# A row of zeros between the parts of queries and keys and the shift, so that two kinds of matmul contract 33 and 35 rows

## The chip, the core and the metric

The kernel runs on one core of one Trainium2 chip. The metric is the device time of one execution in microseconds. The core's engines are TensorE (PE; its weight loads stand in the trace as an engine of their own, PEld), VectorE (DVE), ScalarE (ACT), GpSimd (POOL) and SyncE (SP, which here only issues DMAs). Each works through its own queue in order; they wait for each other by semaphores.

## The reference

One transformer layer: a layer norm, causal attention with 16 heads of 8 dimensions on 8 sequences of 512 tokens, and beside it, on the same normed input, a mixture of 8 experts of which 2 are taken per token, with a shared expert. Everything is float32.

```python
def _L0_attn_ref(x, W1, b1, Wp, bp):
    h = x @ W1 + b1
    h = jnp.swapaxes(h.reshape(B, S, H, 3 * d), 1, 2)
    q, k, v = (h[..., :d], h[..., d:2 * d], h[..., 2 * d:])
    w = jnp.einsum('bhqd,bhkd->bhqk', q, k) / dk
    mask = jnp.tril(jnp.ones((S, S), dtype=x.dtype))
    w = jax.nn.softmax(w * mask - (1.0 - mask) * NEG_BIG, axis=-1)
    a = jnp.einsum('bhqk,bhkd->bhqd', w, v)
    a = jnp.swapaxes(a, 1, 2).reshape(B, S, E)
    return a @ Wp + bp
...
xn = _layernorm(x, axis=-1)
x = x + attn(xn) + (shared expert + the two chosen experts, weighted)(xn)
```

## The kernel before

**Queries and keys.** For a sequence b, `project_qk` makes queries and keys of all heads, each split into a high and a low part (`parts`, L225 and L226), which go through DRAM (`store_qk`) and come back (`fetch`, L259 and L260) into `qs` and `ks`: tiles of 128 partitions in which two heads lie side by side, one from partition 0, one from partition 64 (`SIDE`). Of each head's 64 partitions the first 32 (`QK`) hold the parts: high and low times 8 dimensions, in the order in which one contraction over 32 rows gives the full product. Rows 32 and 33 hold the shift: in `ks` two rows of ones, set once at the start by `memset` on POOL (L137, six of them: three buffers, two heads each); in `qs` the negative row maximum as a high and a low part, written by four DMAs per group of heads (`put_shift`, L394).

**Two passes of scores.** The work is cut into 32 groups (`n`) of four heads and each group into five tiles of scores (`TILES`): two "wide", two "mixed", one "half", which makes 160 steps. In each the same scores are made twice. `peak_scores` (L324, PSUM tile `sc`) contracts the 32 rows of parts; DVE takes the row maxima (L354, L359, L363, L364). `fill` (L278, PSUM tile `scT`) contracts 34 rows with queries and keys swapped, so that transposed scores less the maximum come out; ACT takes the exponential (L405). In each of these two calls two heads are worked on together, one in the array's rows from 0, the other in those from 64. The maxima run nine steps (`AHEAD`) ahead of the exponentials.

The masks: tiles 0 and 2 of the maxima (`MASKED_TILES`) find the mask in PSUM already, copied there by ACT (`prepare`, L312). Of the transposed scores the mask is added on PE (L294) or, in the steps with `on_pool` (from step 25, `BUSY`, until all routed experts are stored), put to zero by POOL after the exponential (L413).

**The order of a step** is written out by hand for PE, DVE, ACT and SP (`manual_schedule`); POOL's order is the framework's. On PE a step goes: `fill` of this step (L278, with L294 where not `on_pool`); `peak_scores` of the step nine further on (L324); a piece of the experts (`extra`: L545, and from `side` L563, L529 and others); and the weighted sums of an earlier tile (`attend`, L428):

```python
waiting.append((kind, j, weigh(n, kind, j, on_pool)))
parts_then = look(step + AHEAD) if step + AHEAD < total_steps else lambda: None
if step not in alone:
    extra()
```

`sc` and `scT` have one buffer each (`m_ps`, `w_ps`).

**The start.** After layer norm of the first sequence and its queries and keys come `project_v(0)`, whose DVE instruction L247 writes the values into `v_ext`, and then the norms of the other sequences. `v_ext` (two tiles) is first set to zero by POOL (L139), and those memsets stand in the program after the ones on `ks`.

Of the kernel before, what the change touches and what calls it, by code (L numbers as in the profile page):

```python
# [10 lines left out]
F32 = mybir.dt.float32  # L11
# [43 lines left out]
QK = 4 * D  # L55
SIDE = 64
# [3 lines left out]
def attn_moe_kernel(  # L60
# [15 lines left out]
    nc = tc.nc  # L76
# [44 lines left out]
    for i in range(NV):  # L121
        t = const.tile([P, NC, H, 32], F32, name=f"v_ext{i}")
# [5 lines left out]
    qs, ks = [], []  # L128
    for i in range(NU):
        q = const.tile([P, HP, S], F32R, name=f"qs{i}")  # L130
        k = const.tile([P, HP, S], F32R, name=f"ks{i}")
        qs.append(q)
        ks.append(k)

    for k in ks:
        for at_ in (QK, SIDE + QK):
            nc.gpsimd.memset(k[at_ : at_ + 2].bitcast(F32), 1.0)  # L137
    for t in v_ext:
        nc.gpsimd.memset(t, 0.0)  # L139
        nc.gpsimd.memset(t[:, :, :, D : D + 1], 1.0)  # L140
# [122 lines left out]
    def rows_of(n, jj, rows):  # L263
        u, i, t = n // 2 % NU, n % 2 * 2 + jj // 2, jj % 2
        at_ = slice(SIDE * t, SIDE * t + rows)
        return qs[u][at_, i, :], ks[u][at_, i, :]
# [4 lines left out]
    def fill(n, kind, j, bare):  # L271

        ps = w_ps.tile([P, 2, S], F32, name="scT")

        def part(out_, jj, width, first):
            q, k = rows_of(n, jj, QK + 2)
            i = NC - width // P
            nc.tensor.matmul(  # L278
                out_, lhsT=k[:, ts(i, P)], rhs=q[:, i * P :], start=first, stop=True,
                skip_group_check=True,  # L280
            )

        if kind == "half":
            blocks = [(u * 2 * P, 2 * P) for u in range(2)]
        else:
            blocks = [(0, S)] if kind == "wide" else [(0, 3 * P), (3 * P, P)]
        for at_, width in blocks:
            for t in range(2):
                jj = (at_ // P if kind == "half" else j) + t
                part(ps[:, t, at_ : at_ + width], jj, width, at_ == 0)  # L290
        if not bare:
            for at_, _ in blocks:
                for t in range(2):
                    nc.tensor.matmul(  # L294
                        ps[:, t, at_ : at_ + P], lhsT=ident16, rhs=mask_k, start=False, stop=True,
                        skip_group_check=True,
                    )
        return ps
# [19 lines left out]
    def peak_scores(n, i):  # L318
        ready_ = bool(ahead)
        ps = ahead.pop() if ready_ else m_ps.tile([P, 2, S], F32, name="sc")  # L320

        def part(at_, jj, c, key, count, start):
            q, k = rows_of(n, jj, QK)
            nc.tensor.matmul(  # L324
                ps[:, jj % 2, ts(at_, P) if count == 1 else ds(at_ * P, count * P)],
                lhsT=q[:, ts(c, P)], rhs=k[:, key * P : (key + count) * P],
                start=start, stop=True, skip_group_check=True,
            )

        j = i // 2 * 2  # L330
        if i == 4:
            blocks = [(0, 0, 2, 0, 2, True), (2, 2, 2, 0, 2, False)]
        elif i in MASKED_TILES:
            blocks = [(c, j, c, c, 1, not ready_ and c == 0) for c in range(NC)]
        else:
            blocks = [(0, j, 3, 0, 3, True), (3, j, 1, 0, 1, False)]
        for at_, jj, *rest in blocks:
            for t in range(2):
                part(at_, jj + t, *rest)
        if i in MASKED_TILES and not ready_:  # L340
            for t in range(2):
                nc.tensor.matmul(
                    ps[:, t].rearrange("p (b k) -> p b k", k=P), lhsT=ident16,
                    rhs=mask_q.unsqueeze(1).to_broadcast([P, NC, P]), start=False, stop=True,
                    skip_group_check=True,
                )
        return ps
# [32 lines left out]
    def shift(n, parts):  # L380

        ps = misc([32, P], "mT_ps")
        nc.tensor.transpose(
            ps, parts.rearrange("p t r i c -> p (t r i c)").bitcast(F32), ident
        )
        mT = at.tile([32, P], F32R, name="mT")
        nc.vector.tensor_copy(mT, ps)
        return partial(put_shift, n, mT)

    def put_shift(n, mT):  # L390
        for t in range(2):
            for r in range(2):
                row = SIDE * t + QK + r
                nc.sync.dma_start(  # L394
                    qs[n // 2 % NU][row : row + 1, ts(n % 2, 2), :].rearrange(
                        "o i (c s) -> o (i c) s", s=P
                    ).bitcast(F32),
                    mT[ts(2 * t + r, 8)].bitcast(F32),
                )
# [631 lines left out]
```

## Time and profile before

| | |
|---|---|
| runs | 672.35 us, the median of 3 (669.31 to 675.39) |
| profiled execution | 672.46 us, of which the span from the first to the last instruction is 670.8 us |
| PE busy | 607.0 us (91%) |
| DVE, ACT, POOL busy | 450.4, 352.7, 223.6 us |
| mean granted PE clock | 0.921 |
| from 130 to 570 us | PE busy 421.02 of 440 us, granted clock 0.98 |

Busy PE includes the time in which a matmul's result is still on its way, so 91% is not a measure of the array's use. In the views, "34*128" is the number of rows that a matmul contracts times the columns of its weights, and "34x384" rows times moving columns. "The chain of work that ended last" is followed back from the last instruction, at each step to what released it.

### The profile page before, as it was taken

The numbers are of one execution on the slowest core, as the hardware profiler recorded it, in microseconds if no ns is written. First come the engines' busy times: TensorE is split into PE (matmuls) and PEld (weight loads), VectorE is DVE, ScalarE is ACT, GpSimd is POOL, SyncE is SP. The second block draws the span as 40 slices with busy tenths as digits, with TensorE's granted clock in tenths as the row PEclk, the third lists the DMA queues.
The fourth block names the chain that finished last, engine by engine and source line by source line (L and its number), as shares of the span: only waits on it lengthen the run. The fifth ranks groups of instructions, "written<-read, shape, count | busy, mean of one in ns | idle before, by whom it ended". The sixth has DMA issues, their size and how long they took to land.

```text
span 670.8 us, 13319 instructions
## 1 busy us (share of the span) xinstructions
PE 607.0 (91%) x4830; PEld 433.9 (65%) x4830; DVE 450.4 (67%) x1059; ACT 352.7 (53%) x582; POOL 223.6 (33%) x325
## 2 busy tenths in 40 slices
PE   3699889998999899998999899989999899989882
PEld 1576657665777577766776677757777677666451
DVE  6547586775777767765776577765777577769643
ACT  3232344554566646665675566664666466535340
POOL 9400077777521111211111112111111111566774
PEclk9556798998999999999999899999999999979986
DMA  8970151416747676657747675857565753111252
GB/s 264 250 203 1 64 171 53 115 53 218 200 159 202 194 208 183 181 178 243 201 148 190 215 194 166 201 194 221 164 178 185 241 160 78 42 47 45 63 136 64
DMA packets 65218, 105.16 MB, mean 157 GB/s; under 512 B 7808, under 2 KB 36224, under 8 KB 65152
## 3 DMA queue, kind: packets, MB, share of 16 engines
q1 hardware_dynamic: 49440, 86.40, 43.2%
q0 software_dynamic: 5344, 13.12, 6.8%
q10 hardware_dynamic: 10368, 4.79, 2.6%
q8 instruction: 39, 0.64, 0.4%
q14 instruction: 27, 0.22, 0.1%
HBM read 71.24 MB, written 32.51 MB: 155 GB/s over the span
## 4 chain that ended last, share of the span: by engine, by line
PE 78%; DVE 10%; ACT 5%; issue 3%; DMA 3%; SPq 0%; DVEq 0%; ACTq 0%
PE gu L545 25%; PE sc L324 12%; PE av L428 11%; PE y L563 11%; PE scT L278 9%; PE lg L734 2%; PE ot L461 2%; ACT th L550 2%; PE scT L294 1%; ACT sc L312 1%; PE s_ps L529 1%; DVE th L551 1%; DMA results<-o 1%; PE qk_ps L224 1%; DVE x_sb L631 1%
## 5 line engine op out<-in xcount | busy, mean ns | idle before, releaser
L405 ACT ACTIVATE pT<-scT 128x1024 f32<-128x1024 f32 x160 | 164.2, 1026 | 125.2 <-PE scT L294 63.9
L413 POOL TENSOR_SCALAR_AFFINE_SELECT pT<-pT 128x256 f32<-128x256 f32 (+1 forms) x156 | 66.3, 438 | 327.9 <-ACT pT L405 324.9
L545 PE MATMUL gu<-sT,w 128*128 128x128 f32 x864 | 125.9, 289 | 2.3 <-PE sc L324 2.1
L359 DVE TENSOR_REDUCE diag<-sc 128x8 f32<-128x1024 f32 x64 | 78.3, 1223 | 66.8 <-PE sc L324 50.5
L545 PEld LDWEIGHTS gu<-sT,w 128*128 128x128 f32 x864 | 105.5, 192 | 14.4 <-PE sc L324 3.5
L550 ACT ACTIVATE th<-gu 128x256 f32<-128x256 f32 x156 | 59.8, 383 | 80.5 <-PE gu L545 78.6
L324 PE MATMUL sc<-ks,qs 32*128 32x128 f32 (+2 forms) x896 | 95.2, 315 | 4.6 <-ACT sc L312 3.5
L551 DVE SCALAR_TENSOR_TENSOR th<-th,gu 128x256 f32<-128x256 f32 x156 | 65.6, 420 | 48.7 <-ACT th L550 48.1
L428 PE MATMUL av<-pT,v_ext 128*32 128x512 f32 (+3 forms) x1024 | 92.4, 457 | 0.0
L278 PE MATMUL scT<-qs,ks 34*128 34x384 f32 (+3 forms) x512 | 83.8, 379 | 6.1 <-ACT pT L405 3.3
L324 PEld LDWEIGHTS sc<-ks,qs 32*128 32x128 f32 x896 | 65.7, 195 | 32.9 <-issue 6.6
L611 POOL DMA_INDIRECT slots<-rows_attT,slot x64 | 62.3, 974 | 72.1 <-DVE slot L822 52.8
L278 PEld LDWEIGHTS scT<-qs,ks 34*128 34x128 f32 x512 | 42.4, 190 | 65.9 <-issue 27.6
L363 DVE TENSOR_REDUCE tops<-sc 128x2 f32<-128x768 f32 x64 | 61.2, 956 | 25.2 <-PE sc L324 25.1
L624 POOL DMA_INDIRECT r<-results,slot x64 | 61.6, 963 | 29.0 <-issue 10.1
L552 DVE TENSOR_TENSOR h<-gu,th 128x256 f32<-128x256 f32 x156 | 66.2, 424 | 5.3
L563 PE MATMUL y<-w,h 128*128 128x128 f32 x432 | 61.3, 278 | 5.6 <-DVE parts L226 3.3
L312 ACT CAST sc<-mask_q 128x1024 f32<-128x1024 bf16 x60 | 61.1, 1019 | 3.3 <-DVE tops L354 2.2
L354 DVE TENSOR_REDUCE tops<-sc 128x4 f32<-128x1024 f32 x32 | 39.2, 1225 | 34.4 <-PE sc L324 34.4
L545 PE MATMUL gu<-xnT,ws_sb 128*128 128x256 f32 x192 | 60.3, 441 | 0.8 <-DVE h L552 0.8
L563 PEld LDWEIGHTS y<-w,h 128*128 128x128 f32 x432 | 54.3, 193 | 9.5 <-PE qk_ps L224 3.9
L545 PEld LDWEIGHTS gu<-xnT,ws_sb 128*128 128x128 f32 x192 | 35.9, 207 | 9.7 <-DVE h L552 1.8
(129 smaller groups left out, 595.9 us busy)
## 6 DMA issues: line engine op xcount, KB each, us to landing
w<-in_w_exp_dram SPq DMA_DIRECT2D x72, 576.0 KB
dq<-parts SPq DMA_DIRECT2D x16, 512.0 KB
dk<-parts SPq DMA_DIRECT2D x16, 512.0 KB
qs<-dq SPq DMA_DIRECT2D x32, 256.0 KB
ks<-dk SPq DMA_DIRECT2D x32, 256.0 KB
slots<-zeros POOLq DMA_DIRECT2D x6, 768.0 KB, 8.1
s<-slots SPq DMA_DIRECT2D x36, 128.0 KB
results<-o ACTq DMA_DIRECT2D x36, 128.0 KB
```

The costliest lines, as they stand in the source:

```text
L278: nc.tensor.matmul(out_, lhsT=k[:, ts(i, P)], rhs=q[:, i * P :], start=first, stop=True, skip_group_check=True,)
L312: nc.scalar.copy(ps.rearrange("p t (b k) -> p (t b) k", k=P), mask_q.unsqueeze(1).to_broadcast([P, 2 * NC, P]),)
L324: nc.tensor.matmul(ps[:, jj % 2, ts(at_, P) if count == 1 else ds(at_ * P, count * P)], lhsT=q[:, ts(c, P)], rhs=k[:, key * P : (key + cou ...
L359: nc.vector.tensor_reduce(diag[:, j : j + 2, :], ps.rearrange("p t (b k) -> p t b k", k=P), AX.X, ALU.max)
L405: nc.scalar.activation(pT, ps, AF.Exp, scale=D**-0.5)
L413: nc.gpsimd.affine_select(out=d, in_=d, pattern=[[0, d.shape[1]], [1, P]], compare_op=ALU.is_ge, fill=0.0, base=0, channel_multiplier=-1,)
L428: nc.tensor.matmul(av[32 * jj : 32 * jj + 32, c * P :], lhsT=v_ext[b % NV][:, c, 4 * g + jj, :], rhs=weights, start=(c == 0), stop=(c == N ...
L545: nc.tensor.matmul(gu[:, i, part], lhsT=w[c][:, ds(i * FP + f * P, P)], rhs=sT[:, part], start=True, stop=True,)
L550: nc.scalar.activation(th, gu[:, 0], AF.Tanh, scale=0.5)
L551: nc.vector.scalar_tensor_tensor(th, th, 1.0, gu[:, 0], ALU.add, ALU.mult)
L552: nc.vector.tensor_tensor(h[:, f], gu[:, 1], th, ALU.mult)
L563: nc.tensor.matmul(y, lhsT=h[:, f, ts(c, P)], rhs=w[c % len(w)][:, ds(2 * FP + f * P, P)], start=(f == 0), stop=(f == NF - 1),)
```

## The change

A row is put between the parts and the shift. It is zero in `ks` and in `qs`. The maxima now contract 33 rows (parts and the row of zeros) and the transposed scores 35 (parts, zeros, two rows of shift). The shift moves one row on. The zeros are written at the start by POOL: for each of the three buffers and two heads, three rows of `ks` get ones, then the first of them zeros, and that row of `qs` zeros.

```diff
-    for k in ks:
+    for q, k in zip(qs, ks):
         for at_ in (QK, SIDE + QK):
-            nc.gpsimd.memset(k[at_ : at_ + 2].bitcast(F32), 1.0)
+            nc.gpsimd.memset(k[at_ : at_ + 3].bitcast(F32), 1.0)
+            nc.gpsimd.memset(k[at_ : at_ + 1].bitcast(F32), 0.0)
+            nc.gpsimd.memset(q[at_ : at_ + 1].bitcast(F32), 0.0)
     for t in v_ext:
         nc.gpsimd.memset(t, 0.0)
         nc.gpsimd.memset(t[:, :, :, D : D + 1], 1.0)
...
         def part(out_, jj, width, first):
-            q, k = rows_of(n, jj, QK + 2)
+            q, k = rows_of(n, jj, QK + 3)
...
         def part(at_, jj, c, key, count, start):
-            q, k = rows_of(n, jj, QK)
+            q, k = rows_of(n, jj, QK + 1)
...
-                row = SIDE * t + QK + r
+                row = SIDE * t + QK + 1 + r
```

## The prediction

> **What bounds the kernel now.** I read the page first, then the chain of waits by windows, then the timelines of PE, its weight loads and POOL.
>
> ```profile
> span 670.8 us, 13319 instructions
> PE 607.0 (91%) x4830; PEld 433.9 (65%) x4830; DVE 450.4 (67%) x1059; ACT 352.7 (53%) x582; POOL 223.6 (33%) x325
> ...
> PE 78%; DVE 10%; ACT 5%; issue 3%; DMA 3%; SPq 0%; DVEq 0%; ACTq 0%
> ...
> L413 POOL TENSOR_SCALAR_AFFINE_SELECT pT<-pT 128x256 f32<-128x256 f32 (+1 forms) x156 | 66.3, 438 | 327.9 <-ACT pT L405 324.9
> ```
>
> PE sets the end over most of the span, so a gap taken out of PE counts there. The 156 selects also count the steps concerned: five tiles need 1+1+2+2+1 = 7 selects, so 156 stand for 111 tiles in which no mask is added on PE. In these the transposed scores (L278) and the maxima (L324) are neighbours on PE: 45 times after a wide tile, 44 after a mixed, 22 after a half one. Such a neighbourhood, first matmuls and then weight loads, in the timeline:
>
> ```profile
> 254.42 0.51 PE L278 MATMUL scT<-qs,ks 34*128 34x384 f32 x4
> 254.86 0.66 PE L324 MATMUL sc<-ks,qs 32*128 32x128 f32 x8
> ...
> 254.42 0.30 PEld L278 LDWEIGHTS scT<-qs,ks 34*128 34x128 f32 x4 [0.84 <-ACT th L550]
> 254.86 0.52 PEld L324 LDWEIGHTS sc<-ks,qs 32*128 32x128 f32 x8
> ```
>
> The four loads of L278 are over in 0.30 us, the last begun at 254.53, while the first pair of matmuls (0.44 us each) still runs: within one kind of matmul, loads run ahead. The first load of L324 comes only at 254.86, 0.33 us after the last load of L278 and 0.15 us after its last matmul began, though what it waits for had long ended: L324's PSUM tile was copied by 254.51. The load has waited for the array to run empty, and PE then stands until it is done.
>
> The start is bound otherwise. The chain there:
>
> ```profile
> 15.05 0.24 DVE rstd L708
> 15.31 0.06 DVE less L709
> 15.38 0.04 issue
> 15.42 0.69 DVE v_ext L247
> 16.11 0.52 DVE rows_attT L724 x2
> 16.63 0.21 DVE stats L701
> 16.87 0.18 DVE mv L702
> ```
>
> From 15 to 23 us the end hangs on DVE, which has no gap of over 0.04 us there. L247 is on it, and L247 writes into the `v_ext` that POOL sets to zero:
>
> ```profile
> 10.64 1.80 POOL L137 MEMSET ks<- 2x2048 f32 x1
> 12.50 3.56 POOL L139 MEMSET v_ext<- 128x2048 f32 x2
> ...
> L137 POOL MEMSET ks<- x6: 1796/1800/1800, 1.1 to 10.6; 2x2048 f32 x6
> ...
> L139 POOL MEMSET v_ext<- x2: 1808/1808/1809, 12.5 to 14.2; 128x2048 f32 x2
> ```
>
> A memset of 2048 elements a partition takes 1.80 us on 2 partitions and 1.81 on 128: the number of rows is free, the number of instructions is not. The first `v_ext` tile is ready at 12.50 + 1.81 = 14.31, so L247 has 15.42 - 14.31 = 1.1 us to spare, less some 0.1 for the signal's way.
>
> **Part one, the boundary on PE: a gain.** With 33 and 35 rows both kinds go into tiles of 64 rows, and I expect loads of L324 to run ahead behind L278 as those inside L278 do. Starts in the trace give the sizes. Loads follow each other in 105 to 112 ns; I take 107. Inside L278 the second pair starts 278 ns after a first of 384 columns and 218 after one of 256, each with its exposed load: 128 columns cost about 57, and a first pair of 512 would be followed after some 332. From the last L278 to the first L324 the median is 428 ns after a wide tile, 149 after a mixed (last pair 128 columns) and 205 after a half one (256 columns), and then comes the exposed load. Without the drain it would be 332, 110 (the pace of loads) and 114, the load hidden. So the savings are:
>
> - wide: 428 + 107 - 332 = 203 ns, 45 times: 9.1 us
> - mixed: 149 + 107 - 110 = 146 ns, 44 times: 6.4 us
> - half: 205 + 107 - 114 = 198 ns, 22 times: 4.4 us
>
> Together 19.9 us. Not all is on the path. At 9 places the chain runs elsewhere, mostly through ACT's copy of the mask for the first tile of a group, as here:
>
> ```profile
> 262.88 0.38 ACT th L550
> 263.27 0.93 ACT sc L312
> 264.19 0.04 issue
> 264.24 0.66 PE sc L324 x8
> ```
>
> That takes 9 times about 0.19, 1.7 us. At most other first tiles this copy ends about 0.2 us before the load, which the saving uses up exactly; some 0.7 us more may go there and at the pauses between sequences. I take **17.5 us**; bounds 13 (one boundary in three covered by another wait) and 20; that nothing comes is a rival below.
>
> The Trainium skill has a rule for this and one against it. "TensorEngine Tiling (Array Packing)", Key Properties, says that a change of tiling mode, not of tile alone, drains TensorE; the 0.15 us above agree. "TensorE: Matmul & The Clock Gate", Part 3 (The mechanism), says that a weight load overlaps matmuls in flight only where its row group differs. By that sentence L324's load, in the row groups that L278 has just used, would wait after the change too, and the sum would lose its whole gain. The trace speaks against it: L278's second pair loads into the rows of its first pair while that one runs.
>
> **Part two, the memsets: a loss.** Six become eighteen. The rows to be zeroed in `ks` are first set to one, then to zero, and `qs` adds its own: twelve more. POOL's memsets start 1.834 us apart (at 8.806 and 10.640), so POOL reaches `v_ext` 12 x 1.834 = 22.0 us later, if it goes on taking its instructions in the order of the program, as it did: all of L137 before L139, save for one short select. L247 then starts at 36.4 instead of 15.4. Behind it in DVE's queue stand the norms and statistics of all further sequences (L724, L701), behind those PE's transposes (L728), the gate (L734) and the first maxima (L324 at 28.30). The parts of the first queries and keys are not behind it, and what they would hide is small: their fetch lands at about 26.2, and now waits. The chain passes L247, so the delay reaches the end in full: 22.0 - 1.0 = **21.0 us**. Bounds: 19 (the framework places a `v_ext` memset one instruction earlier) and 22.1. The masks, `zeros` and the clearing DMAs (L691, which now begin near 40 in place of 26.23) are late too, but their users are behind L247 as well. The rows of the first buffer are ready near 12 us, long before the first maxima.
>
> **Part three, small things.** Matmuls of 33 and 35 rows cost what those of 32 and 34 do: a pair of 256 columns is followed after 218 ns in L278 and in L324. From L278 to the mask's matmul (L294) the gap after 128 columns is 150 ns, from L324 to L545 it is 143 to 146: some 4 ns more for the tile of 64 rows, 150 times, 0.5 us. The four DMAs of the shift stay four, of the same size, on SP in the same place; only their row moves, and nothing new waits for them. The 39 places where the masking matmul stands between L278 and L324 still change mode.
>
> **The sum**, against the profiled execution of 672.46 us (670.8 of it span; the median of the runs, 672.35, is the same within their spread): 672.5 - 17.5 + 21.0 + 0.5 = **676.5 us**. About 1% either way is what a measurement of this kernel can tell from no change.
>
> **The rivals.**
>
> - *POOL gets `v_ext` done in time*: its order is not written by hand and the memsets on late buffers could be put behind. For it: the third buffer is needed only later. Against it: POOL kept the order of the program before. Then 672.5 - 17.5 + 0.5 = 655.5 us.
> - *The boundary still drains*: 33 and 35 rows differ, as 32 and 34 did, or loads into row groups in use don't run ahead across two kinds. For it: no row shows two different counts of rows side by side without a drain. Against it: L278 itself. It decides if L324's first load still starts 0.15 us after L278's last matmul of 128 columns. Then 672.5 + 21.0 = 693.5 us, slower.
> - *The ring of the maxima's one PSUM buffer takes over*: maxima, DVE's reduction (1.22 us), ACT's copy (1.02), maxima. For it: six first tiles wait for it already, and most others have 0.2 us left. Against it: the tiles in the middle of a group have 0.3 to 2 us left. It decides where the copy ends later than the hidden load could start. If all 23 first tiles and the mixed ones with under 0.3 us lost their savings (about 23 x 0.2 + 5 x 0.15), and as much again were lost by what shifts behind, the gain would be 19.9 - 10.7, some 9, and the time 672.5 - 9 + 21.5 = 685 us.
>
> **How the numbers follow.** I give my forecast 0.78, the rivals 0.09, 0.07 and 0.06. The forecast's own bounds are 672.5 + 19 - 20 = 671.5 and 672.5 + 22.1 + 0.5 - 13 = 682; with the spread of the runs 669 to 684 holds nearly all of it and half of the last rival, about 8 in 10. Faster by over 1% (under 665.6) is the first rival and a small part of the forecast: 0.11. Slower by over 1% (above 679.1) is the last two rivals and an eighth of the forecast: 0.23. The rest, 0.66, lies within 1%.
>
> **What would show it.** Right: eighteen memsets on POOL up to about 34 us; L247 near 36.4 and the first L324 near 49; a load of L324 that begins before L278's last matmuls end; PE's stretch from 130 to 570 shorter by 17 to 18 us. The start is wrong if L247 stays near 15; the gain is wrong if the gaps from L278 to L324 stay at 428, 149 and 205 ns, or if new waits for L312 appear ahead of L324.

## The result, and the profile after

The change made the kernel slower by about 1%: the ratio to the kernel before is 1.0104, with a 95% interval of 1.0065 to 1.0142, which is 672.34 x 1.0104 = 679.3 us. In a second set of runs it was 1.0132 (1.0051 to 1.0213). The ratio takes the fast runs of each kernel alone, those within 1.5% of its fastest; the plain median of all 20 runs of the changed kernel is 687.09 us (673.15 to 696.68), 2.2% above that of the kernel before, since many of its runs were granted a lower clock, on which more is said at the end.

The profiled execution took 683.4 us. In all listings of this kernel the line numbers are two higher than before, so L326 is the maxima, L280 the transposed scores, L547 gate and up, L249 the values, L141 the memset of `v_ext`.

```profile
span 681.7 us, 13331 instructions
PE 588.9 (86%) x4830; PEld 435.7 (64%) x4830; DVE 451.0 (66%) x1059; ACT 352.4 (52%) x582; POOL 244.2 (36%) x337
...
PE 70%; DVE 9%; POOL 6%; ACT 5%; issue 4%; DMA 4%; POOLq 0%; SPq 0%; ACTq 0%; DVEq 0%
```

PE is busy 18.1 us less and POOL 20.6 us more, and POOL now has a share in the chain that ended last. The chain at the start shows where:

```profile
28.22 1.80 POOL ks L137
30.02 1.75 POOL qs L139
31.77 1.76 POOL ks L138
33.52 0.05 issue
33.57 1.82 POOL v_ext L141
35.41 0.69 DVE v_ext L249
36.10 0.52 DVE rows_attT L726 x2
```

The values are written at 35.41 in place of 15.42. All eighteen memsets run ahead of `v_ext`, DVE's queue stands behind L249, and the first maxima begin at 48.28 in place of 28.30: 19.98 us.

The boundary that the prediction showed at 254.42 (a mixed tile), now; matmuls, then weight loads:

```profile
269.60 0.50 PE L280 MATMUL scT<-qs,ks 35*128 35x384 f32 x4
269.94 0.61 PE L326 MATMUL sc<-ks,qs 33*128 33x128 f32 x8
...
269.60 0.30 PEld L280 LDWEIGHTS scT<-qs,ks 35*128 35x128 f32 x4 [0.84 <-ACT th L552]
269.88 0.52 PEld L326 LDWEIGHTS sc<-ks,qs 33*128 33x128 f32 x8
```

The maxima's load starts 0.28 us after the first one of the transposed scores, before 0.44. It now starts together with the last pair of matmuls of the transposed scores (both at 269.88), where before it came 0.15 us after that pair had begun. Over all neighbours, the median from the last L280 to the first L326 fell from 428 to 337 ns after a wide tile, from 149 to 57 after a mixed one and from 205 to 115 after a half one, and the load of 107 ns behind it is now hidden, after a mixed tile about half of it (there the steps below become 140 to 146 ns shorter in all). So both halves of the change did what the forecast said of them. What is less than forecast is what came of the hidden drains in the total.

### The profile page after: what moved, and what is told of

Its sections match the earlier page's. It is cut to its first block, busy times and chain, and to the rows that moved or that the text cites. A ratio compares the mean times of both kernels' runs of the same rounds, so it can differ in the third digit from the quotient of the medians.

```text
span 681.7 us, 13331 instructions
## 1 busy us (share of the span) xinstructions
PE 588.9 (86%) x4830; PEld 435.7 (64%) x4830; DVE 451.0 (66%) x1059; ACT 352.4 (52%) x582; POOL 244.2 (36%) x337
## 4 chain that ended last, share of the span: by engine, by line
PE 70%; DVE 9%; POOL 6%; ACT 5%; issue 4%; DMA 4%; POOLq 0%; SPq 0%; ACTq 0%; DVEq 0%
PE gu L547 23%; PE av L430 10%; PE y L565 10%; PE sc L326 9%; PE scT L280 8%; DMA r<-results,slot 2%; PE lg L736 2%; PE ot L463 2%; POOL ks L137 2%; POOL ks L138 2%; POOL qs L139 2%; DMA results<-o 1%; ACT th L552 1%; ACT sc L314 1%; PE scT L296 1%
## 5 line engine op out<-in xcount | busy, mean ns | idle before, releaser
L547 PE MATMUL gu<-sT,w 128*128 128x128 f32 x864 | 128.1, 293 | 6.3 <-PE sc L326 4.7
L547 PEld LDWEIGHTS gu<-sT,w 128*128 128x128 f32 x864 | 107.8, 196 | 19.3 <-PE sc L326 10.1
L326 PE MATMUL sc<-ks,qs 33*128 33x128 f32 (+2 forms) x896 | 88.0, 299 | 4.3 <-ACT sc L314 3.5
L280 PE MATMUL scT<-qs,ks 35*128 35x384 f32 (+3 forms) x512 | 84.1, 378 | 7.4 <-DMA qs<-mT 3.8
L430 PE MATMUL av<-pT,v_ext 128*32 128x512 f32 (+3 forms) x1024 | 90.3, 449 | 0.0
L280 PEld LDWEIGHTS scT<-qs,ks 35*128 35x128 f32 x512 | 42.4, 189 | 65.8 <-issue 29.0
L326 PEld LDWEIGHTS sc<-ks,qs 33*128 33x128 f32 x896 | 69.7, 200 | 15.0 <-ACT sc L314 6.1
L626 POOL DMA_INDIRECT r<-results,slot x64 | 61.4, 960 | 25.1 <-issue 10.7
L547 PE MATMUL gu<-xnT,ws_sb 128*128 128x256 f32 x192 | 58.4, 430 | 1.0 <-DVE h L554 1.0
L547 PEld LDWEIGHTS gu<-xnT,ws_sb 128*128 128x128 f32 x192 | 35.1, 203 | 9.5 <-DVE h L554 1.9
```

What stands on the lines that cost most here:

```text
L280: nc.tensor.matmul(out_, lhsT=k[:, ts(i, P)], rhs=q[:, i * P :], start=first, stop=True, skip_group_check=True,)
L326: nc.tensor.matmul(ps[:, jj % 2, ts(at_, P) if count == 1 else ds(at_ * P, count * P)], lhsT=q[:, ts(c, P)], rhs=k[:, key * P : (key + cou ...
L430: nc.tensor.matmul(av[32 * jj : 32 * jj + 32, c * P :], lhsT=v_ext[b % NV][:, c, 4 * g + jj, :], rhs=weights, start=(c == 0), stop=(c == N ...
L547: nc.tensor.matmul(gu[:, i, part], lhsT=w[c][:, ds(i * FP + f * P, P)], rhs=sT[:, part], start=True, stop=True,)
```

## The experiments

The first set (the next four runs) fell on a chip on which the kernel before took 775.24 us: the sends of the tokens to the experts landed later there (in the runs of this set the first load of slots is issued at 239 to 267 us, in the profile before at 168.9). What is compared is the ratios within a set, and the lengths of steps that lie outside that stretch. The other sets had 675.93 and 674.37 us for the kernel before.

**The late memsets.** Only the first buffer's rows are set first; the others follow POOL's other work.

```diff
-    for q, k in zip(qs, ks):
+    def ones_and_zeros(q, k):
         for at_ in (QK, SIDE + QK):
             nc.gpsimd.memset(k[at_ : at_ + 3].bitcast(F32), 1.0)
             nc.gpsimd.memset(k[at_ : at_ + 1].bitcast(F32), 0.0)
             nc.gpsimd.memset(q[at_ : at_ + 1].bitcast(F32), 0.0)
+    ones_and_zeros(qs[0], ks[0])
...
     nc.gpsimd.memset(zeros, 0.0)
+    for i in range(1, NU):
+        ones_and_zeros(qs[i], ks[i])
```

> The changed kernel, with the memsets on the rows of the second and third buffer put behind POOL's other work at the start (after the memset of zeros); those of the first buffer stay first, so six memsets lie ahead of v_ext, as before the change. Theory (the start lost some 20 us because L247 waited for the memset of v_ext, and the steady part gained 11 to 14): the write of the values on DVE starts near 15.4 us again, the first maxima at 28.3, and the time is 657 to 663 us, a ratio of 0.975 to 0.987 to the kernel before. Rival (the start was slow for another reason, or the 33 and 35 rows gain nothing once the start is out of the way): 670 us or more.

The ratio was 0.9898 (0.9847 to 0.9949), 7.9 us of 775, less than was expected. Run twice more:

> The late memsets again, beside the change itself on the same chip. Theory: 20 us faster than the change, 8 to 13 us faster than the kernel before. Rival (the granted clock falls as PE waits more, and takes back the steady gain): within 3 us of the kernel before.

> The late memsets a third time, for its interval. Theory: a ratio of 0.98 to 0.99 to the kernel before, 8 to 12 us, with the start at 28.4 us. Rival (no gain once the granted clock is counted): 0.995 to 1.005.

The second time gave medians of 671.77 us against 675.93 for the kernel before, 4.2 us, with a spread too wide for a ratio (659.66 to 672.75), and against 685.74 for the change beside it; the third gave 661.74 us and a ratio of 0.9836 (0.9785 to 0.9887), 11 us. Its chain at the start and POOL's rows (here L251 writes the values, L143 is `v_ext`):

```profile
15.09 0.24 DVE rstd L714
15.46 0.69 DVE v_ext L251
16.15 0.55 DVE rows_attT L730 x2
```

```profile
10.39 1.80 POOL L138 MEMSET ks<- 1x2048 f32 x1
12.25 3.56 POOL L143 MEMSET v_ext<- 128x2048 f32 x2
...
17.86 0.19 POOL L684 MEMSET zeros<- 128x128 f32 x1
18.12 1.80 POOL L137 MEMSET ks<- 3x2048 f32 x1
```

The eighteen memsets are all still there, and POOL is busy 244.3 us as with the change; the write of the values is back at 15.46 and the first maxima at 28.37. The start is free, and what the rows are worth alone is seen: about 8 to 11 us by the two ratios (with their intervals 4 to 14.5). This version is faster than the kernel before by 1.0 and 1.6% in these two sets.

**The memsets alone**, in the kernel before:

```diff
+    for q, k in zip(qs, ks):
         for at_ in (QK, SIDE + QK):
             nc.gpsimd.memset(k[at_ : at_ + 2].bitcast(F32), 1.0)
+            nc.gpsimd.memset(k[at_ : at_ + 1].bitcast(F32), 1.0)
+            nc.gpsimd.memset(q[at_ : at_ + 1].bitcast(F32), 0.0)
```

> The kernel before (32 and 34 rows) with twelve more memsets of 2048 elements on POOL in the same places as in the change; the contractions are untouched. Theory: the first maxima start at 48.3 us instead of 28.3 and the whole 20 us come through to the end: 690 to 695 us, a ratio of 1.027 to 1.034. Rival (part of the delay at the start is caught up later, since PE, DVE and the DMA queues have slack after 60 us): 675 to 685 us.

The ratio was 1.0259 (1.0202 to 1.0316): 20.1 us of 775.24. The microseconds are those of the slower chip; the difference is what was expected, and the view of DVE at the start names the cause:

```profile
35.40 0.69 DVE L249 TENSOR_TENSOR v_ext<-v_ps,bv_sb 128x512 f32<-128x512 f32 x1 [19.91 <-POOL v_ext L141]
```

As far as this interval tells (15.7 to 24.5 us), nothing of it is caught up in the 750 us that follow: where the clock is full, steps 25 to 134 are as long as in the kernel before, with medians within 1 ns. With the late memsets both parts of the change have now been measured apart: +20 and -8 to -11 make +9 to +12, against +7.0 and +8.9 from the two ratios of the whole change.

**Where the rest of the drains went.** I compared the two traces step by step, taking for each step from 25 to 135 the time from one transposed tile's first matmul to the next one's, and leaving out steps at a halved clock. The medians (changed less before): after the first wide tile -192 ns, the second wide -187 (but zero in 8 of 21), the first mixed -140 (but five of 18 became longer, by 129 to 183), the second mixed -146, the half tile -8 (only 5 of 22 reach -170 or more). The half tiles' 198 ns had gone nearly everywhere. One such step, before, PE and then DVE:

```profile
217.73 0.50 PE L278 MATMUL scT<-qs,ks 34*128 34x256 f32 x4
218.16 0.50 PE L324 MATMUL sc<-ks,qs 32*128 32x384 f32 x4
219.01 0.57 PE L545 MATMUL gu<-sT,w 128*128 128x128 f32 x3 [0.36 <-PE sc L324]
...
218.03 0.42 DVE L551 SCALAR_TENSOR_TENSOR th<-th,gu 128x256 f32<-128x256 f32 x1 [0.20 <-ACT th L550]
218.49 0.43 DVE L552 TENSOR_TENSOR h<-gu,th 128x256 f32<-128x256 f32 x1
```

and with the change:

```profile
234.11 0.51 PE L280 MATMUL scT<-qs,ks 35*128 35x256 f32 x4
234.45 0.40 PE L326 MATMUL sc<-ks,qs 33*128 33x384 f32 x4
235.40 1.13 PE L547 MATMUL gu<-sT,w 128*128 128x128 f32 x8 [0.55 <-PE sc L326]
...
234.41 0.42 DVE L553 SCALAR_TENSOR_TENSOR th<-th,gu 128x256 f32<-128x256 f32 x1 [0.21 <-ACT th L552]
234.87 0.42 DVE L554 TENSOR_TENSOR h<-gu,th 128x256 f32<-128x256 f32 x1
```

The maxima start 0.34 us into the step where they started 0.43, but gate and up start 1.29 us into it both times, 0.1 us after DVE's last operation on the previous piece (218.92 and 235.29). The wait before them has grown from 0.36 to 0.55 us, just the saving. The view puts it down to the maxima, which had long ended; by the times it is DVE. The buffer `gu` exists once, and the ring matmul, tanh, two DVE operations, matmul takes the whole saving.

One half tile's step became much longer, step 79, the last of the fourth sequence: by 2.9 us in the changed kernel, at a full clock. The next transposed scores there wait for the DMAs of the shift (`put_shift`, now L396), of which SP issued three late:

```profile
380.12 2.01 SPq L396 DMA_DIRECT2D qs<-mT  x3
382.04 0.47 PE L280 MATMUL scT<-qs,ks 35*128 35x512 f32 x1 [2.91 <-DMA qs<-mT]
```

In the kernel before, the same matmul at 364.28 found no wait. Over all profiles of this document this wait is 1.3 to 3.8 us in the eight with 33 and 35 rows (mean 2.3) and 0 to 1.5 us in the five with 32 and 34 (mean 0.6), so some 1.7 us of the gain end here. SP issued the first of the four at 373.10 and the second only 7.0 us later, before the change 4.3 us later; what held it was not tried.

**A shorter ring.** The first DVE operation left out, with the late memsets and in the kernel before:

```diff
-        nc.vector.scalar_tensor_tensor(th, th, 1.0, gu[:, 0], ALU.add, ALU.mult)
```

> As the run with the late memsets, but DVE's first operation on the gate and up products (the one that makes x(1+tanh) of tanh) is left out, so that the output is not the reference's. This shortens the ring of the one gate-and-up PSUM buffer (matmul, tanh, two DVE operations, next matmul) by about 0.45 us a step. To be read against the kernel before with the same operation left out. Theory (the ring took the savings at 17 half tiles and some others): against that kernel the rows now save 16 to 18 us, as counted by boundaries. Rival (something else than the ring takes the savings): 10 to 13 us, as with the ring whole.

> The kernel before with DVE's first operation on the gate and up products left out (output not the reference's): the reference for the run above. Theory: PE sets the end in most steps, so it is only 2 to 8 us faster than the kernel before, about 665 to 670 us. Rival (the ring already bounds many steps before the change): 655 us or less.

In time this is open: 754.9 us (ratio 0.9742, 0.9691 to 0.9794) and 771.44 us (0.9863, 0.9802 to 0.9924). The medians lie 16.5 us apart, the ratios 9.4, and the spread of the second kernel is too wide to tell 16 from 11. The steps are clear: between these two the half tiles' steps are shorter by some 186 ns (184 to 196, once 320) in 15 of 22 and by about 72 in 6 (the last one is step 79, 0.9 us longer), and the first mixed ones -143, none of them longer. A half tile's step of the shorter ring:

```profile
293.54 0.51 PE L282 MATMUL scT<-qs,ks 35*128 35x256 f32 x4
293.88 0.40 PE L328 MATMUL sc<-ks,qs 33*128 33x384 f32 x4
294.33 0.94 PE L549 MATMUL gu<-sT,w 128*128 128x128 f32 x6
```

Gate and up start 0.79 us into it instead of 1.29. The ring is what took the half tiles' savings. The second wide tile's stayed lost in 8 of 20 steps, so these have another cause. In the two traces of before and after the change it is, in six of the eight, the one that the prediction named: the maxima wait for ACT's copy of the mask and start 0.67 us into the step both times. In the other two they start earlier (0.34 us in place of 0.43), and the saving is lost behind them; by what, is open.

**One PSUM tile for all pieces**, with the late memsets and in the kernel before, in the hope that the next gate half would wait only for the readers of the old gate half:

```diff
+    gu = gu_ps.tile([P, 2, PAIR], F32, name="gu")
+
     def chunk(k, f):
...
-        gu = gu_ps.tile([P, 2, PAIR], F32, name="gu")
```

> The late memsets, and the gate-and-up PSUM tile made once for all chunks instead of taken anew for each, so that the matmuls of the next gate half wait only for the operations that read the old gate half, and not for the last one on the up half. All of the computation is done. Theory (the savings at the half tiles went into the ring of this buffer): the half tiles' steps become about 0.19 us shorter than with the kernel before and the same split, and the time is 5 to 8 us below that of the late memsets alone. Rival (the ring is bound by its chain through ACT and DVE and not by the last read; or only the leaving out of work helped): the same as the late memsets alone, within 2 us.

> The kernel before with the gate-and-up PSUM tile made once for all chunks: the reference for the run above. Theory: the ring bound few steps before the change, so 0 to 4 us faster than the kernel before. Rival (the ring was a bound before the change as well): 6 us or more faster, and the rows then save no more than they did with the ring whole.

The kernel before didn't change: 1.0046 (0.9999 to 1.0093). With the late memsets it was 663.75 us, a ratio of 0.9807 (0.9708 to 0.9905). But the edit did not do what it was for:

```profile
216.11 0.40 PE L328 MATMUL sc<-ks,qs 33*128 33x384 f32 x4
217.01 0.38 PE L550 MATMUL gu<-sT,w 128*128 128x128 f32 x1 [0.50 <-DVE h L557]
```

PE still waits for DVE's last operation, only the way of the signal is some 50 ns shorter; the half tiles' steps are 70 ns shorter in the median, not 190. As DVE does the same work here as with the ring whole, these 70 ns speak for the ring, and against the rival to the reading of the shorter ring, that a DVE with less to do was what helped. In time, the interval overlaps that of the late memsets alone, so which of the two is the faster is open.

**The up half copied by ACT**, so that DVE's last operation reads no PSUM:

```diff
-        nc.vector.tensor_tensor(h[:, f], gu[:, 1], th, ALU.mult)
+        nc.scalar.copy(h[:, f], gu[:, 1])
+        nc.vector.tensor_tensor(h[:, f], h[:, f], th, ALU.mult)
```

> The late memsets, and ACT copies the up half out of PSUM right after its tanh of the gate half, so that DVE's last operation reads no PSUM and the gate-and-up buffer is free one DVE operation (0.42 us) earlier. All of the computation is done; ACT gets 156 copies of some 0.38 us more, 59 us. Theory (the half tiles' savings went into this ring): the steps of the half tiles become some 0.19 us shorter than in the kernel before with the same copies, as in the run that left an operation out. In time this may be lost again where ACT's copy of the mask for the first tile comes later. Rival (leaving the operation out helped by unloading DVE, not by the ring): the half tiles' steps stay within 0.02 us.

> The kernel before with the up half copied by ACT: the reference for the run above. Theory: within 1% of the kernel before; if ACT's 59 us more delay the copies of the mask, up to 10 us slower.

Far worse than expected: 712.07 us (1.0562, 1.0493 to 1.0631) with the late memsets, 728.64 us (1.0811, 1.0746 to 1.0876) in the kernel before. The waits of the latter:

```profile
ACT h L552 <- DVE th L551: 84.4, 156, 1.7
...
PEld sc L324 <- ACT sc L312: 39.3, 47, 2.7
```

All 156 copies waited for DVE's first operation instead of running beside it, 84.4 us in which ACT's queue stood, and the copies of the mask behind them came late for PE. It tells one thing nevertheless: between these two kernels the second wide tile's steps save nothing in 16 of 16, the second mixed ones nothing either in most. There the ring of the maxima's buffer binds, and it takes the drains just as the other ring does. The half tiles' steps save 124 ns in the median against 8, which agrees with a ring partly freed.

## Why the prediction was right or wrong

**The time**, 676.5 us forecast, 679.3 by the ratio, within the range, and 1.04% slower: on the line between "within 1%", which I held likeliest, and "slower by over 1%". The main statement held, that a gain on PE and a loss of much the same size at the start come together, with the loss the greater. That the time fell into the range owes something to its width: the gain was 6.5 to 9.5 us too large, and only 1.0 us of this was made up by a loss that was too large as well.

**The start** was right in mechanism and nearly in size: 20.0 us instead of 21.0. The memsets start 1.78 us apart on average (1.75 to 1.85) rather than 1.834, so that `v_ext` begins 21.1 us later, less 1.1 us to spare. POOL kept the program's order, so the first rival fell. That the delay reaches the end whole, which I read from one row of the chain, is shown by the memsets alone: 20.1 us.

**The drain** was right in mechanism: the load runs ahead between 33 and 35 rows, though its row groups are those just in use. The sentence of "TensorE: Matmul & The Clock Gate", Part 3 (The mechanism), that loads overlap only where the row group differs, taken by itself, does not hold here; what "TensorEngine Tiling (Array Packing)", Key Properties, says of a change of tiling mode agrees with the gaps of 149 ns before and 57 after. The second rival fell. One of the signs given could not tell, though: before the change the load (254.86), too, began ahead of the end that the view gives for the matmuls in front of it (254.93). What tells is that it no longer begins 0.15 us after the last of them.

**What failed is the term "17.5 us, bounds 13 and 20".** The three savings per boundary were well sized (192, 140 to 146 and, with the ring shortened, 186 ns, where I had 203, 146 and 198). Wrong was what I took off: only 9 boundaries, because I asked where the chain leaves PE *at* the boundary, and looked for covers only at the instruction next to it. I did not ask what PE waits for after it. At the half tiles PE waited 0.36 us before gate and up already, and a saving ahead of a longer wait is worth nothing: 17 times 0.198 = 3.4 us. The ring of the maxima took 6 savings, about as I had it, and five of the first mixed tiles' steps became longer by up to 0.18 us, which the shorter ring undid. By the two ratios of the late memsets the gain is 8 to 11 us, below my lower bound of 13, which one of the two intervals still reaches. (The neighbourhoods were also miscounted by one: 46 after a wide tile and 112 in all, worth 0.2 us.) The third rival had the right kind of cause, a ring of a single PSUM buffer, but the wrong ring; the one it named binds wholly only in the kernels with ACT's extra copies.

The sign of a stretch shorter by 17 to 18 us failed with this term. From the start of step 25 to that of step 135 (173.6 to 566.9 us before) the two profiles differ by only 2.9 us: 99 steps at a full clock gained 10.7, step 79 lost 2.9, and the ten steps with a halved clock in either profile lost 4.9, with 27.3 us halved in this stretch in place of 10.2. Outside the first stretch at the start, the two profiles have nearly the same halved time in all (61.9 and 63.2 us).

The 0.5 us for longer drains after the maxima are too little for the times to show; in the traces the gap from the maxima to gate and up, after 128 columns, went from 199 to 201 ns in the median. That nothing new waits for the shift's DMAs was wrong at one place, step 79 above.

## What to carry to other kernels

A drain between two kinds of matmul, of 32 and of 34 rows, was taken away here by a row of zeros that made them 33 and 35. Before counting such savings, follow PE past each place to its next wait: where it stands there for a ring of single buffers, or for a transfer, the saving only lengthens that wait. And an instruction added at the start costs its time in full where a queue in order stands behind it on the chain: here the place of twelve memsets, not their number, decided between 1% slower and 1.0 to 1.6% faster.

## What the runs showed that I had not expected

The span follows the granted clock closely: over the 20 runs of the changed kernel from 671.4 us at a mean clock of 0.925 to 695.0 at 0.885. In the traces the clock is either full or halved, and the halved stretches, but for the last, which the end cuts off, are multiples of 3.4 us (3.4, 6.8, 10.2 and 61.4 us in the changed kernel's profile). The four in the middle of that run start in the first three steps of a sequence, and PE had been idle for 25 to 50% of the 6.8 us before each of them. With the longer start the first halved stretch is 61.4 us instead of 44.4 in these two profiles, while PE's busy time in it is nearly the same (36.2 and 37.0 us). Why the changed kernel was granted less in so many runs was not settled.

In the kernel before with the up half copied, ACT's copy out of one half of a PSUM tile waited for DVE's operation on the other half in every one of 156 cases; whether the chip or the framework's bookkeeping asks for that was not tried.
